# One change to a transformer layer on one core: later groups' normed x transposed by blocks, TensorE at work on ones while x loads, fewer first loads, stores in the residual's order, states 256 wide

## The chip, the core and the metric

The kernel runs on one core of one Trainium2 chip. The core has five engines with a queue each: TensorE (matmuls, written PE in the profile, its weight loads PEld), VectorE (DVE), ScalarE (ACT), GpSimd (POOL) and SyncE (SP), which here only issues DMAs. TensorE writes to PSUM[...]; all other data is in SBUF or in DRAM. The metric is the device time of one launch in microseconds. Before the change the median of 3 runs is 1242.43 us (1240.35 to 1243.34).

## The reference

One layer of attention and one feed-forward block work on the same normed x, and both are added to x. B, T, D = 8, 256, 256, with H = 16 heads of 128, M = 64 states per head, and an MLP of 2048 whose weights come as 4-bit codes with scales.

```python
xn = layernorm(x)                                   # 8 x 256 x 256
# attention
q, k = rope(xn @ Wq.T), rope(xn @ Wk.T);  v = xn @ Wv.T
s = clip(xn @ Ws1.T @ Ws2.T + bs2, -32, 32)         # low rank: 256 -> 16 -> 16 heads x 64 states
z = cumlogsumexp(s, over time);  es, enz = exp(s), exp(-z)
A = where(causal, q @ k.T * scale, 0)
ok = enz * (A @ es);  qv = softmax(ok, over states)
W2 = where(causal, (qv * enz) @ es.T, 0)
o = W2 @ v
o = o * rsqrt(mean(o * o) + eps) * g_norm_weight * silu(xn @ Wg.T)
attn = o @ Wo.T
# feed-forward
gate, up = xn @ dequant(gate_W).T, xn @ dequant(up_W).T
ffn = (gelu_tanh(gate) * up) @ dequant(down_W).T
return x + attn + ffn
```

All arithmetic is in float32.

## The kernel before

The 2048 tokens are cut into four groups of 512 (two sequences each, `g`). A step `n` is one group and one pair of heads, so there are 32 steps, run in order; a step takes about 36 us. While step n's scores, values, gates and logits are made, step n - 1 is finished (its cross terms, weights, outputs) and step n + 1 is prepared (rope and states). The feed-forward block is spread over all steps: `ffn` (L430) is a generator that gives, for each quarter of the MLP and each group, four pairs of gate and up blocks (L370, L376 and L398) and then two down products (L423).

The order on each engine is written out by a planner inside the kernel. For each step the functions are put on a list with a place in the step (`POS`, `START` for the first steps), and called in that order; a call issues its TensorE instructions at once, and hands the work of the other engines to a chain. A small clock model (`advance`, L114) with estimated durations decides in which order the chains' pieces are issued on VectorE, ScalarE, GpSimd and SyncE. `DUE` says how many pieces of the MLP's weights are unpacked by which step, `FIRST` and `LAST` how much feed-forward work the first and last steps get. None of this waits at run time: what runs is five fixed queues, each in order, tied by semaphores.

Names and lines that matter here:

- `norm` (L244): mean and variance on VectorE (L254, L255, L256), the power -1/2 on GpSimd (L258), z = normed x (L261). It is done in two halves per group, of 256 tokens each.
- `norm_turn` (L272): four transposes of a half on TensorE against the identity (L279), copied by ScalarE into xT (L289). xT is what all projections read. `NORMS` says in which step a later group is normed: group 1 in step 0, group 2 in step 2, group 3 in step 5. Group 2 and 3's x is loaded by `load_x` at the start of their step.
- `low_rank` (L481, matmuls L487) and `states` (L499, matmuls L515). rT holds four copies of the 16 low-rank rows and a row of ones in the four quarters of the partitions, and w_s2 four copies of the weights with the bias row, so four matmuls with 17 rows each can run beside each other. Each of four PSUM banks gets two matmuls of 128 columns. VectorE clips them into esT and es (L526).
- `rope` (L548, matmuls L556), `value` and `gate` (`vg`, L605, matmuls L613), `scores` (L632, L635), `logits` (L652), `softmax` (L672).
- `turned` (L450): a transpose of blocks. VectorE transposes 32x32 blocks (L453), four DMAs write the blocks to their places in DRAM (L457, `by_way`), and one DMA reads them back (L462). It is used for ok, its softmax and the outputs.
- `cross` (L723, copied by L732), `weights` (L748, masked into wt by L758), `apply` (L775, reads what L732 copied), `outputs` (L791), `close` (L841). `weights` and `apply` are two entries of the list, at 0.182 and 0.257 of a step.
- `add_to` (L345): adds a product to the residual `res` (L349). After the last addition to two tiles of 128 tokens it stores them, by eight DMAs of 32 KB (L356), since x was loaded with its rows in another order than the output's.
- The first loads, on two queues: x in two parts, the first projection weights, ws1, one_at, cos, sin and four copies of w_s2, of 17 rows each (L224 to L232); the packed weights of the MLP follow (L303, L304).

## Time and profile before

| what | value |
|---|---|
| median of 3 runs | 1242.43 us |
| the profiled execution | 1241.07 us |
| its span, first to last instruction | 1239.3 us |
| mean granted TensorE clock | 0.988 |
| first TensorE instruction | 7.10 us |
| end of the last addition to the residual | 1233.26 us |
| L556, L613, L376, L398, L423, L841 (128 x 128 weights) | 248.7, 237.0, 121.2, 123.1, 122.0, 115.7 us busy |
| DMA | 115.15 MB, mean 93 GB/s |

The profile is of one execution. Busy times of matmuls overlap a little, since they are pipelined; from one start to the next a pass of 512 columns takes 0.43 us in the middle of the run and one of 128 columns 0.107. Each float32 matmul shows as two passes (the count behind x), a transpose as one. A line such as `PE ps L279 <- DVE z L261: 16.8, 3, 7.1` says that TensorE sat idle before its instructions of line 279 for 16.8 us in all, 3 times, 7.1 us at most, until an instruction of VectorE at line 261 that writes z was done.

### The profile page before, as it was taken

To read this page: it belongs to the slowest core of one execution; us is meant where nothing else is said; L and a number is where in the kernel's file an instruction comes from. 1 tells how busy PE (TensorE), PEld (TensorE's weight loads), DVE (VectorE), ACT (ScalarE), POOL (GpSimd) and SP (SyncE) were. 2 spreads that over 40 slices of the span, in tenths; PEclk is the share of its full clock that TensorE was granted. 3 is DMA by queue.
4 is the path that set the end of the run, shared out by engine and by line. 5 is a ranking of instruction groups with operands and counts; after the bars stand their busy time and mean duration, and the time that the engine had idled before them with its cause. 6 is when DMAs were issued, how large, how long until landed. Compare 5 with 4: busy or idle time off the path is not lost.

```text
span 1239.3 us, 18558 instructions
## 1 busy us (share of the span) xinstructions
PE 1202.6 (97%) x6192; PEld 838.2 (68%) x6192; DVE 891.9 (72%) x1720; ACT 516.0 (42%) x1653; POOL 484.7 (39%) x440
## 2 busy tenths in 40 slices
PE   6899899999999999999999999899999999999996
PEld 3466586766767667767776676676766767667774
DVE  4988668868686887767777777777677586776643
ACT  3335335444354443543444443345434354442430
POOL 3525444424244433434443343444244344433310
PEclk9989999999999999999999999899999999999998
DMA  5234332324343233333332334322233333333322
GB/s 157 86 103 120 95 110 75 107 58 119 96 118 94 62 85 93 103 101 96 108 85 80 94 86 119 85 77 83 63 103 102 86 102 85 90 83 102 86 69 51
DMA packets 111495, 115.15 MB, mean 93 GB/s; under 512 B 13156, under 2 KB 83172, under 8 KB 111400
## 3 DMA queue, kind: packets, MB, share of 16 engines
q1 hardware_dynamic: 110968, 113.71, 34.2%
q8 instruction: 49, 0.80, 0.3%
q14 instruction: 46, 0.38, 0.1%
q10 hardware_dynamic: 432, 0.26, 0.1%
HBM read 78.27 MB, written 35.65 MB: 92 GB/s over the span
## 4 chain that ended last, share of the span: by engine, by line
PE 86%; DVE 9%; DMA 2%; issue 1%; POOL 1%; ACT 0%; POOLq 0%; DVEq 0%; SPq 0%; ACTq 0%
PE ps L556 16%; PE ps L613 15%; PE ps L423 9%; PE ps L841 9%; PE ps L376 8%; PE ps L398 7%; PE ps L632 4%; PE ps L791 4%; PE ps L652 4%; PE ps L748 3%; PE ps L635 2%; PE ps L515 2%; PE ps L775 1%; DVE enz L543 1%; DMA pk<-in_codes_dram 1%
## 5 line engine op out<-in xcount | busy, mean ns | idle before, releaser
L571 POOL TENSOR_TENSOR z<-z,sin 128x512 f32<-128x512 f32 x128 | 165.6, 1294 | 370.8 <-ACT z L567 369.5
L556 PE MATMUL ps<-xT,wts 128*128 128x512 f32 x512 | 248.7, 609 | 0.5 <-ACT xT L289 0.5
L613 PEld LDWEIGHTS ps<-wts,xT 128*128 128x128 f32 x1024 | 194.3, 190 | 64.1 <-issue 37.6
L613 PE MATMUL ps<-wts,xT 128*128 128x256 f32 x1024 | 237.0, 379 | 0.2
L556 PEld LDWEIGHTS ps<-xT,wts 128*128 128x128 f32 x512 | 92.1, 192 | 79.6 <-issue 69.8
L423 PE MATMUL ps<-w_down,inter 128*128 128x256 f32 x512 | 122.0, 392 | 9.4 <-DVE inter L407 7.4
L695 ACT ACTIVATE ok<-okT,mx 128x64 f32<-128x64 f32 x256 | 85.6, 337 | 91.2 <-DVE mx L689 86.6
L398 PE MATMUL ps<-xT,w_up 128*128 128x512 f32 x256 | 123.1, 604 | 0.0
L376 PE MATMUL ps<-xT,w_gate 128*128 128x512 f32 x256 | 121.2, 596 | 0.0
L572 POOL TENSOR_TENSOR q<-q,z 128x512 f32<-128x512 f32 x64 | 81.5, 1273 | 94.8 <-DVE q L569 69.7
L423 PEld LDWEIGHTS ps<-w_down,inter 128*128 128x128 f32 x512 | 98.9, 196 | 26.4 <-DVE inter L407 9.7
L841 PE MATMUL ps<-w_o,ogT 128*128 128x256 f32 x512 | 115.7, 379 | 0.0
L349 DVE TENSOR_TENSOR res<-ps,res 128x512 f32<-128x512 f32 x64 | 44.0, 688 | 93.9 <-PE ps L423 57.7
L841 PEld LDWEIGHTS ps<-w_o,ogT 128*128 128x128 f32 x512 | 96.5, 190 | 20.5 <-issue 8.1
L543 DVE RECIPROCAL enz<-enz 128x128 f32<-128x128 f32 x128 | 108.5, 909 | 0.0
L817 DVE SCALAR_TENSOR_TENSOR og<-ps,ss,sgate 128x128 f32<-128x128 f32 x256 | 75.3, 344 | 45.9 <-POOL ss L813 45.9
L566 ACT COPY z<-ps 64x512 f32<-64x512 f32 x128 | 74.5, 582 | 73.0 <-PE ps L556 63.8
L813 POOL TENSOR_TENSOR ss<-ss,nhalf 128x4 f32<-128x4 f32 x64 | 65.0, 1017 | 91.6 <-DVE ss L809 90.5
L572 POOL TENSOR_TENSOR k<-k,z 128x512 f32<-128x512 f32 x64 | 82.6, 1290 | 20.6 <-DVE k L569 16.9
L385 POOL TENSOR_SCALAR t<-t 128x512 f32<-128x512 f32 x64 | 40.7, 637 | 119.7 <-ACT t L383 116.2
L389 ACT ACTIVATE t<-t 128x512 f32<-128x512 f32 x64 | 40.2, 629 | 108.1 <-DVE t L387 108.0
L623 DVE TENSOR_TENSOR at<-ps,mask 128x384 f32<-128x384 f32 x128 | 65.4, 552 | 26.4 <-PE ps L635 26.0
(76 smaller groups left out, 1904.7 us busy)
## 6 DMA issues: line engine op xcount, KB each, us to landing
wts<-in_wqkvg_dram SPq DMA_DIRECT2D x64, 512.0 KB, 4.1
by_way<-ok SPq DMA_DIRECT2D x256, 64.0 KB, 1.8
okT<-by_way SPq DMA_DIRECT2D x64, 256.0 KB, 2.7
by_way<-og SPq DMA_DIRECT2D x256, 64.0 KB, 2.2
ogT<-by_way SPq DMA_DIRECT2D x64, 256.0 KB, 3.7
pk<-in_codes_dram SPq DMA_DIRECT2D x12, 256.0 KB, 4.3
sc<-in_scales_dram SPq DMA_DIRECT2D x12, 256.0 KB, 4.1
w_o<-in_wo_dram SPq DMA_DIRECT2D x4, 512.0 KB, 7.4
```

Source lines behind the costliest of these rows:

```text
L376: nc.tensor.matmul(pg, lhsT=w_gate[:, c, ns], rhs=xT[:, c, gs], start=c == 0, stop=c == 1)
L398: nc.tensor.matmul(pu, lhsT=w_up[:, c, ns], rhs=xT[:, c, gs], start=c == 0, stop=c == 1)
L423: nc.tensor.matmul(ps[:, k, :], lhsT=inter[g, n][0][:, (i + k) * P : (i + k + 1) * P], rhs=w_dn[:, n, :], start=n == 2 * q, stop=n == 2 * ...
L543: nc.vector.reciprocal(r, r)
L556: nc.tensor.matmul(ps, lhsT=w[:, c, :], rhs=xT[:, c, g * G : (g + 1) * G], start=c == 0, stop=c == 1)
L566: nc.scalar.copy(z[0:64], pv[64:128])
L571: nc.gpsimd.tensor_tensor(z, z, sin_b, ALU.mult)
L572: nc.gpsimd.tensor_tensor(y, y, z, ALU.add)
L613: nc.tensor.matmul(ps[:, k, :], lhsT=xT[:, c, tt], rhs=w[:, which, c, :], start=c == 0, stop=c == 1,)
L695: nc.scalar.activation(pr[:, js, i, :], okT[:, js, i, :], AF.Exp, bias=mx[:, k : k + 1], scale=SCALE, accum_out=sm[:, k : k + 1],)
L817: nc.vector.scalar_tensor_tensor(og[:, :, k, :], po[:, k, :].rearrange("p (c k) -> p c k", c=4), ss[:, k : k + 1], sg[:, k, j * DK : (j + ...
L841: nc.tensor.matmul(ps[:, k, :], lhsT=ogT[hh][0][:, i + k], rhs=w_o[:, (hp // 2) * 4 + hh, :], start=hh == 0, stop=hh == 3,)
```

## The change

- Only group 0 is still transposed on TensorE. The norm of groups 1 to 3 writes its result in blocks (four VectorE instructions of half the width in place of two), VectorE transposes the blocks, and six DMAs take them through DRAM into xT: four into `by_way`, two out of it. `turned` is split, and its first part, `scattered`, serves both. The norm stands earlier in its step (`NORM_AT`).
- VectorE sets `ones` first, and 18 matmuls of ones by ones stand ahead of all else on TensorE. Nothing reads their result.
- The first loads: ws1, one_at and gw come as one tensor (`small`), cos and sin as one (`turns`), and w_s2 as one of 128 rows, its four copies laid out on the host. All are on SP's queue.
- A store is one DMA of 256 KB: the output keeps the order of the residual's rows, and the host puts the rows in order.
- `states` makes two matmuls of 128 columns for two of the four banks, and one of 256 columns for each of the other two.
- `apply` is called at the end of `weights`, and no longer at a place of its own.
- The planner's places, due times and shares are other ones.

In the built program TensorE has 3042 matmul instructions in place of 3112 (24 transposes and 64 matmuls of states fewer, 18 on ones more), and SP issues 8 stores in place of 64 and 36 DMAs more for the six halves of the later norms; the first use of a later group's xT is the first L376 of that group, as before.

```diff
@@ -28,32 +28,33 @@
 SCALE = DK ** -0.5
 GELU_C = 0.7978845608028654
 GELU_A = 0.044715
-
-
-POS = {'scores': (0.057, 0.067),
+WARM = 18
+
+
+POS = {'scores': (0.053, 0.063),
  'logits': (0.14,),
- 'softmax': (0.303,),
+ 'softmax': (0.301,),
  'cross': (0.15,),
- 'weights': (0.182, 0.257),
- 'low': (0.024,),
+ 'weights': (0.169,),
+ 'low': (0.046,),
  'states': (0.167,),
- 'outputs': (0.364, 0.398),
+ 'outputs': (0.364, 0.472),
  'close': (0.348, 0.396),
  'rope': (0.197, 0.336, 0.411, 0.543),
- 'vg': (0.502, 0.566, 0.766, 0.838)}
-START = {-1: {'states': (0.437,), 'rope': (0.143, 0.267, 0.533, 0.633)},
- 0: {'vg': (0.0, 0.03, 0.06, 0.076),
-     'scores': (0.115, 0.195),
-     'states': (0.403,),
-     'logits': (0.318,),
+ 'vg': (0.502, 0.663, 0.838, 0.869)}
+START = {-1: {'states': (0.437,), 'rope': (0.128, 0.358, 0.518, 0.588)},
+ 0: {'vg': (0.0, 0.03, 0.076, 0.214),
+     'scores': (0.082, 0.162),
+     'states': (0.386,),
+     'logits': (0.216,),
      'softmax': (0.433,),
-     'rope': (0.198, 0.211, 0.24, 0.458)}}
-FEED = {-1: (0.301, 1.0)}
+     'rope': (0.211, 0.24, 0.245, 0.458)}}
+FEED = {-1: (0.244, 1.0)}
 NORMS = {0: 1, 2: 2, 5: 3}
-NORM_AT = (0.366, 0.78, 0.889, 0.92)
-FIRST = [0.29, 1.41]
-LAST = [1.6, 1.98]
-DUE = [4, 6, 7, 7, 8, 9, 10, 10, 11, 12, 12, 13, 14, 15, 15, 16, 17, 17, 18, 19, 19, 22, 23, 23, 24]
+NORM_AT = (0.204, 0.465)
+FIRST = [0.29, 1.5]
+LAST = [1.49, 1.82]
+DUE = [4, 6, 7, 7, 8, 9, 10, 11, 11, 11, 12, 13, 14, 15, 15, 16, 17, 17, 18, 19, 19, 22, 23, 23, 24]
 
 
...
@@ -181,13 +182,13 @@
     mask = const.tile([P, 3 * P], F32, tag="mask", name="mask")
     tri, ones = mask[:, 0:P], mask[:, P : 2 * P]
     nhalf = const.tile([P, TC], F32, tag="nhalf", name="nhalf")
-    cos = const.tile([P, T], F32, tag="cos", name="cos")
-    sin = const.tile([P, T], F32, tag="sin", name="sin")
-
-    w_s1 = const.tile([P, 2, P], F32, tag="w_s1", name="w_s1")
+    turns = const.tile([P, 2, T], F32, tag="turns", name="turns")
+    cos, sin = turns[:, 0], turns[:, 1]
+
+    small = const.tile([P, 258], F32, tag="small", name="small")
+    w_s1 = small[:, 0:256].rearrange("p (c f) -> p c f", c=2)
+    one_at, gw = small[:, 256:257], small[:, 257:258]
     w_s2 = const.tile([P, H * M], F32, tag="w_s2", name="w_s2")
-    one_at = const.tile([P, 1], F32, tag="one_at", name="one_at")
-    gw = const.tile([P, 1], F32, tag="gw", name="gw")
     w_o = const.tile([P, H, D], F32, tag="w_o", name="w_o")
     w_gate = const.tile([P, 2, MLP], F32, tag="w_gate", name="w_gate")
     w_up = const.tile([P, 2, MLP], F32, tag="w_up", name="w_up")
@@ -221,17 +222,14 @@
             wts[n, k] = w
             loads((n, k), 512)
 
+    nc.vector.memset(ones, 1.0)
     load_x(0, 2)
     load_x(2, 2)
-    nc.scalar.dma_start(out=w_s1.rearrange("p c f -> p (c f)"), in_=a["ws1"])
     load_w(0, 0)
-    nc.scalar.dma_start(out=one_at, in_=a["one_at"])
-    nc.scalar.dma_start(out=cos, in_=a["cos"])
-    nc.sync.dma_start(out=sin, in_=a["sin"])
-    for r in range(0, P, 32):
-        nc.sync.dma_start(out=w_s2[r : r + 17, :], in_=a["ws2"])
+    nc.sync.dma_start(out=small, in_=a["small"])
+    nc.sync.dma_start(out=turns.rearrange("p k t -> p (k t)"), in_=a["turns"])
+    nc.sync.dma_start(out=w_s2, in_=a["ws2"])
     make_identity(nc, ident)
-    nc.gpsimd.memset(ones, 1.0)
     make_upper_triangular(nc, mask[:, 0:P])
     make_upper_triangular(nc, mask[:, 2 * P : 3 * P])
     nc.gpsimd.memset(nhalf, -0.5)
@@ -256,16 +254,39 @@
             nc.vector.tensor_scalar(rstd, mv[:, :, 1], EPS, None, ALU.add)
             yield "g", 1.0
             nc.gpsimd.tensor_tensor(rstd, rstd, nhalf[:, 0:2], ALU.pow)
-            yield "v", 0.9
+            if g == 0:
+                yield "v", 0.9
+                for i in range(2):
+                    nc.vector.tensor_scalar(
+                        xn[:, i, :], res[:, g * TC + h + i, :], mv[:, i, 0:1],
+                        rstd[:, i : i + 1], ALU.subtract, ALU.mult,
+                    )
+                return
+
+            bl = xn.rearrange("p i d -> p (i d)").rearrange("p (q c r k) -> p q c r k", q=4, c=2, r=2)
             for i in range(2):
-                nc.vector.tensor_scalar(
-                    xn[:, i, :], res[:, g * TC + h + i, :], mv[:, i, 0:1],
-                    rstd[:, i : i + 1], ALU.subtract, ALU.mult,
-                )
-
-        xns[g, h] = xn, chain(
-            work(), st, mv, rstd, xn, rank=0, at=landed["x", g * TC + h]
-        )
+                yield "v", 0.6
+                for c in range(2):
+                    nc.vector.tensor_scalar(
+                        bl[:, :, c, i, :],
+                        res[:, g * TC + h + i, c::2].rearrange("p (q k) -> p q k", q=4),
+                        mv[:, i, 0:1], rstd[:, i : i + 1], ALU.subtract, ALU.mult,
+                    )
+            by_way = yield from scattered(bl.rearrange("p q c r k -> p q (c r) k"))
+            yield "d", 0.8, 4.2
+            for c in range(2):
+                nc.sync.dma_start(
+                    out=xT[:, c, g * G : (g + 1) * G].rearrange("p (i x) -> p i x", i=4)[
+                        :, :, 32 * h : 32 * h + 64
+                    ],
+                    in_=by_way[:, :, 64 * c : 64 * (c + 1)],
+                )
+
+        c = chain(work(), st, mv, rstd, xn, rank=0, at=landed["x", g * TC + h])
+        if g == 0:
+            xns[g, h] = xn, c
+        else:
+            normed.setdefault(g, []).append(c)
 
     xns = {}
 
@@ -349,13 +370,11 @@
         nc.vector.tensor_tensor(r, ps, r, ALU.add)
         done[t] = done.get(t, 0) + 1
         if done[t] == left:
-            yield "d", 0.9
-            for k in (t, t + 1):
-                rows = out[k // TC * G : (k // TC + 1) * G].rearrange("(i r k) d -> r i k d", i=4, r=4)
-                for i in range(4):
-                    nc.sync.dma_start(
-                        out=rows[k % TC, i], in_=res[32 * i : 32 * (i + 1), k, :]
-                    )
+            yield "d", 0.4
+            nc.sync.dma_start(
+                out=out[t * P : (t + 2) * P, :].rearrange("(i p) d -> p i d", p=P),
+                in_=res[:, t : t + 2, :],
+            )
 
     def decoded(k):
 
@@ -447,8 +466,8 @@
 
 
 
-    def turned(to, t):
-        yield "v", 0.8
+    def scattered(t):
+        yield "v", 0.7
         flat = t.rearrange("p c i k -> p (c i k)")
         nc.vector.transpose(flat, flat)
         yield "d", 1.75, 2.6
@@ -458,17 +477,16 @@
                 out=by_way.rearrange("(c k) r x -> r k c x", c=4)[r],
                 in_=t[32 * r : 32 * (r + 1)].rearrange("p c i k -> p c (i k)"),
             )
+        return by_way
+
+    def turned(to, t):
+        by_way = yield from scattered(t)
         yield "d", 0.4, 4.2
         nc.sync.dma_start(
             out=to.rearrange("p r i k -> p (r i k)"), in_=by_way.rearrange("p r x -> p (r x)")
         )
 
-    def blocks_of(t):
-
-        return t.rearrange("p (i c k) -> p c i k", i=TC, c=4)
-
     def load_wo():
-        nc.sync.dma_start(out=gw, in_=a["gw"])
         for h in range(0, H, 4):
             nc.sync.dma_start(out=w_o[:, h : h + 4, :], in_=a["wo"][:, h : h + 4, :])
 
@@ -506,15 +524,20 @@
         esT = to["esT"] = new(p2, [P, G], "esT", 2)
 
         pss = [bank() for _ in range(4)]
+        toks, sts = [rT[32 * r : 32 * r + 17] for r in range(4)], [w_s2[32 * r : 32 * r + 17, ms] for r in range(4)]
         for i in range(2):
             for r, ps in enumerate(pss):
-                rows = slice(32 * r, 32 * r + 17)
-                k = 2 * (r % 2) + i
-                tok, st = rT[rows, k * P : (k + 1) * P], w_s2[rows, ms]
-                lhsT, rhs = (tok, st) if r < 2 else (st, tok)
-                nc.tensor.matmul(
-                    ps[:, i * P : (i + 1) * P], lhsT=lhsT, rhs=rhs, start=True, stop=True
-                )
+                if r < 2:
+                    k = 2 * r + i
+                    nc.tensor.matmul(
+                        ps[:, i * P : (i + 1) * P], lhsT=toks[r][:, k * P : (k + 1) * P],
+                        rhs=sts[r], start=True, stop=True,
+                    )
+                elif i == 0:
+                    nc.tensor.matmul(
+                        ps[:, 0:T], lhsT=sts[r], rhs=toks[r][:, (r - 2) * T : (r - 1) * T],
+                        start=True, stop=True,
+                    )
 
         enz = to["enz"] = new(p2, [P, G], "enz", 2)
 
@@ -760,6 +783,7 @@
                 )
 
             to["wt", j] = wt, chain(work(), wt, pss[j], rank=0)
+        apply(n)
 
     def apply(n):
 
@@ -849,6 +873,10 @@
     banks = NG * (MLP // P * 2 + 8)
     weight = FIRST + [1.0] * (N + 2 - len(FIRST) - len(LAST)) + LAST
     feeding = ffn()
+
+    ps = bank()
+    for _ in range(WARM):
+        nc.tensor.matmul(ps[:, 0:P], lhsT=ones, rhs=ones, start=True, stop=True)
     for m in range(2):
         load_packed(m)
     load_w(0, 2)
@@ -869,10 +897,11 @@
         def put_norm(g, places):
             for k, h in enumerate((0, 2)):
                 put_at(places[k], norm, g, h)
-                put_at(places[2 + k], norm_turn, g, h)
 
         if n == -1:
-            put_norm(0, (0.0, 0.0, 0.1, 0.1))
+            put_norm(0, (0.0, 0.0))
+            for h in (0, 2):
+                put_at(0.1, norm_turn, 0, h)
             put_at(0.2, low_rank, 0)
         if n + 1 < N:
             if n >= 0 and steps[n][1] == 7:
@@ -902,7 +931,6 @@
         if n > 0:
             put("cross", 0, cross, n - 1)
             put("weights", 0, weights, n - 1)
-            put("weights", 1, apply, n - 1)
             for k in range(2):
                 put("outputs", k, outputs, n - 1, k)
             if n % 2 == 1 and n > 1:
@@ -961,18 +989,20 @@
     cos, sin = _tables()
     n = {k: np.asarray(v) for k, v in x.items()}
     at, ff = "L0_attn_", "L0_ffn_"
+    ws1 = n[at + "Ws1"].T.reshape(P, 2, 1, 16)
+    ws1 = np.pad(ws1, [(0, 0)] * 3 + [(0, 16)]).repeat(4, 2).reshape(P, 256)
+    bias = (np.arange(P) % 32 == 16).astype(np.float32).reshape(P, 1)
+    ws2 = np.concatenate([n[at + "Ws2"].T, n[at + "bs2"].reshape(1, H * M)])
+    ws2 = np.pad(ws2, [(0, 15), (0, 0)])
     return {
         "x": c(n[at + "hidden_states"].reshape(NG, 4, 4, 32, D).swapaxes(1, 2).reshape(NTOK, D)),
         "wqkvg": pairs([n[at + w] for w in ("Wq", "Wk", "Wv", "Wg")]),
         "wo": c(n[at + "Wo"].T.reshape(H, DK, D).transpose(1, 0, 2)),
-        "ws1": c(np.pad(n[at + "Ws1"].T.reshape(P, 2, 1, 16), [(0, 0)] * 3 + [(0, 16)]).repeat(4, 2).reshape(P, 256)),
-        "one_at": (np.arange(P) % 32 == 16).astype(np.float32).reshape(P, 1),
-        "ws2": c(np.concatenate([n[at + "Ws2"].T, n[at + "bs2"].reshape(1, H * M)])),
-        "gw": c(n[at + "g_norm_weight"].reshape(DK, 1)),
+        "small": c(np.concatenate([ws1, bias, n[at + "g_norm_weight"].reshape(DK, 1)], 1)),
+        "ws2": c(np.concatenate([ws2] * 4)),
         "codes": quarters(lambda w: w, "_W_packed"),
         "scales": quarters(lambda w: w.repeat(16, 0), "_scales"),
-        "cos": c(cos),
-        "sin": c(sin),
+        "turns": c(np.concatenate([cos, sin], 1)),
     }
 
 
@@ -990,4 +1020,5 @@
     with tile.TileContext(nc) as tc:
         layer_kernel(tc, aps, out)
     r = run_bass_kernel_spmd(nc, [arrays], core_ids=[0])
-    return r.results[0]["out_0_dram"].reshape(B, T, D)
+    o = r.results[0]["out_0_dram"].reshape(NG, 4, 4, 32, D).swapaxes(1, 2)
+    return np.ascontiguousarray(o).reshape(B, T, D)
```

## The prediction

> **What bounds the kernel now.** I read the page's busy times first, then the waits of TensorE, then the timeline of TensorE at each wait, and last the end of the run. The page gives the bound and the share of it:
>
> ```profile
> PE 1202.6 (97%) x6192; PEld 838.2 (68%) x6192; DVE 891.9 (72%) x1720; ACT 516.0 (42%) x1653; POOL 484.7 (39%) x440
> ```
>
> From about 80 us to 1212 us TensorE has almost no gap: there only fewer or cheaper TensorE instructions pay. What is lost beside that is in a few places, and the waits of TensorE name them (us in total, times, longest):
>
> ```profile
> PE ps L279 <- DVE z L261: 16.8, 3, 7.1
> PE ps L423 <- DVE inter L407: 7.4, 5, 2.6
> PE ps L515 <- DMA w_s<-in_ws_dram: 2.2, 1, 2.2
> ```
>
> The timeline of TensorE shows where (start, length, line; behind it the idle time before):
>
> ```profile
> 7.10 2.25 PE L279 MATMUL ps<-ident,z 128*128 128x128 f32 x8 [7.10 <-DVE z L261]
> 9.81 3.78 PE L556 MATMUL ps<-xT,wts 128*128 128x512 f32 x4 [0.46 <-ACT xT L289]
> ...
> 63.58 1.23 PE L279 MATMUL ps<-ident,z 128*128 128x128 f32 x4 [5.15 <-DVE z L261]
> ...
> 139.58 1.09 PE L279 MATMUL ps<-ident,z 128*128 128x128 f32 x4 [4.58 <-DVE z L261]
> ```
>
> TensorE stands in order, so a transpose whose z is late holds all behind it. Each long wait also slows the clock afterwards: four passes over 512 columns take 1.72 us from start to start in the middle of the run, but 3.58 us at 9.81 and 3.41 us at 64.61; the windows give a granted clock of 0.78 between 57.80 and 73.55 us and 0.84 between 134 and 145 us.
>
> **Part by part.**
>
> *Start.* Before, TensorE is first busy at 7.10 us. 18 matmuls on ones (36 passes of 128 columns) now run from about 1 us, after one memset on VectorE. What does the clock make of them? The row: first work at 7.10, half speed in every pass until about 13.9 us, so some 6.8 us of work with gaps. [...] A slow pass is 0.214 us and a fast one 0.107 (half and full rate of the 0.43 us per 512 columns). [...] by the row near 1.0 + 6.8 + 4 x 0.107 = 8.2 us, which makes the first transposes 1 us late. The second half's z ends at 8.38 either way, so both lead to a first L556 at about 9.4 (0.4 earlier) and fast from there. I take the row's side for the finish and full speed after it: 0.4 + 3.58 - 1.72 = 2.3 us, and some 0.4 of L487.
>
> The w_s2 load is now one of 128 rows and not four of 17. Those four hold SP's queue: its rows show it waiting 2.9, 2.6, 2.6 and 2.5 us for them, one after the other, and the packed weights issued behind them at 5.24 us reach VectorE only at 20.36. The new loads ahead of L515 are 1.9 MB; at the 221 to 267 GB/s of the first 10 us, an estimate of 9 us for w_s2 and 11 us for the first packed weights (2.2 MB and its scales). So the 2.2 us wait at 19.87 goes, with the slow clock behind it. By TensorE's own work the states then end at 9.4 + 4 passes + 4 passes (L487) + 4 passes + 0.65 = 15.2 us and not 20.48.
>
> What is late next is VectorE. From 20.36 to 73.5 us it is busy almost throughout (15.43 of 15.57 us, then 21.51 of 21.75, then 15.48 of 15.75), and 73.5 is when the fourth inter lets the first L423 run. Its order in the changed program has the same work before that point, plus two stream transposes (0.70 each) and smaller norm pieces (about 0.6): 2 us more. It comes to the clip of esT (before: 22.57) at 15.3, 7.2 us earlier. So the first L423 moves by 7.2 - 2.0 = 5.2 us. The 5.15 us wait at 63.58 goes as a wait on L279 but comes back as waits on VectorE inside this stage. If VectorE were no bound, TensorE's sum would allow about 15. **I take 5**, bounds 2 and 15.
>
> *Group 2's transpose.* At 139.58 the wait (4.58) and the slow clock (L632 1.06 against 0.60, and a clock of 0.84 over 11 us: 1.8) go: 6.4 at most. xT comes by VectorE, SP and DRAM; its readers are gate blocks of a later step, and the program's only waits on these DMAs stand at the first L376 of each group. VectorE has 47 of 60 us busy before it, so 1.4 + 0.6 us more can hide, but not all of the time won: **5.5**, bounds 3 and 6.4. The transposes themselves: group 3 shows 254.32 to 255.27, 0.95 us without a wait, so **1.9** for groups 2 and 3.
>
> [...] xT is now written in runs of 256 B. The near rows: okT<-by_way, 256 KB in 2 KB runs, lands in 2.7 us, by_way<-ok, 64 KB in 512 B runs, in 1.8. By the row 128 KB costs about 2 us[...]; the first reader of group 1 is at 96.04 before, and z of its second half is there at 63.8. [...] It costs elsewhere: in SP's queue the four z and two xT issues stand ahead of okT (0.44 each), so the first softmax comes some 3 us later. prT of step 0 was done at 75.5 and wanted at 78.45; I count 0, bound 3 lost.
>
> *apply joined to weights.* Not in the change's name, but in its diff, and it meets every step. Before, another matmul group stands between L748 and L775, except once at the end:
>
> ```profile
> 1164.14 1.16 PE L748 MATMUL ps<-prT,esT 64*128 64x128 f32 x16
> 1165.24 1.98 PE L398 MATMUL ps<-xT,w_up 128*128 128x512 f32 x4
> 1167.15 0.71 PE L775 MATMUL ps<-cross,prT 64*128 64x128 f32 x8
> 1167.80 3.72 PE L841 MATMUL ps<-w_o,ogT 128*128 128x256 f32 x16
> ...
> 1199.87 1.16 PE L748 MATMUL ps<-prT,esT 64*128 64x128 f32 x16
> 1200.86 0.61 PE L775 MATMUL ps<-cross,prT 64*128 64x128 f32 x8
> 1201.41 1.98 PE L398 MATMUL ps<-xT,w_up 128*128 128x512 f32 x4
> ```
>
> Apart, from start to start: 1.10 + (1.91 - 1.72) + 0.65, and 0.1 in the group behind: 2.05. Together: 0.99 + 0.55 + 0.1 = 1.64. So 0.41 us a step, 31 times: 12.7. But the order makes a new wait. The L556 behind the joined pair takes a PSUM bank that the first esT clip frees, and this clip waits for the last L748, because esT is overwritten:
>
> ```profile
> 1133.36 1.16 PE L748 MATMUL ps<-prT,esT 64*128 64x128 f32 x16
> ...
> 1134.60 0.76 DVE L526 TENSOR_SCALAR esT<-ps 128x256 f32<-128x256 f32 x2 [0.77 <-PE ps L748]
> ```
>
> The clip starts 1.24 after L748 and takes 0.42: free at 1.66, seen by TensorE at about 1.73, where the joined pair is through at 1.53. So 0.2 us of wait in 30 steps, with all of TensorE queued behind: 12.7 - 6.1 = **6.6**. Bounds: 12.7 if the wait is absorbed, 0 if VectorE comes 0.4 later. ACT's copy of cross ends 0.17 us before L748 starts, so L775 itself waits for nothing.
>
> *States 256 wide.* Two of four row groups take one matmul of 256 columns for two of 128; the groups run beside each other[...]. Columns per group stay: 0, bounds -3 and +3 over 32 steps.
>
> *Positions and due times.* At 792 us TensorE waits 1.93 and 1.95 us for VectorE before L423, and runs slow after (L423 x10 takes 4.49 instead of about 2.2). Before, this down stood 2.56 us of TensorE work behind its last up block; in the changed order it stands 5.1. A later one falls from 11.1 to 2.56. I take **3**, bounds 0 and 5. The last down still follows its up block at once, so the 3.7 us of waits at 1213 to 1217 stay.
>
> *Stores.* The end:
>
> ```profile
> 1229.83 7.31 SPq L356 DMA_DIRECT2D out_dram<-res  x16
> 1232.57 0.69 DVE L349 TENSOR_TENSOR res<-ps,res 128x512 f32<-128x512 f32 x1 [2.76 <-PE ps L841]
> ```
>
> The last sum ends at 1233.26, eight issues of 0.45 follow, and the last lands 1.6 us after its issue: 6.0 us to the end. One store of 256 KB takes one issue and lands in 2.7 to 4 us (okT, ogT, x of that size): 3.1 to 4.5. **2.3 gained**, bounds 1.5 and 2.9. Earlier stores end beside TensorE work.
>
> *Sum:* 5 + 5.5 + 1.9 + 6.6 + 0 + 3 + 2.3 = 24.3 us. The profiled execution took 1241.07 us (span 1239.3), which gives 1216.8; the runs' median is 1242.43, 1.4 above. I predict **1217**.
>
> **Rivals.**
> 1. *VectorE is no bound in the first 70 us.* Then the start gives some 13 and not 5, and the rest stays: 1209. For it: part of VectorE's busy time there is stretched (L328 x4 in 3.72 us, 0.25 each at best), which may not recur. Against it: three windows at 98 to 99%. Chance 0.22.
> 2. *The joined pair pays nothing,* since the clip's wait eats the 0.41: 1224. For it: VectorE often has another 0.68 us operation between the transpose of ok and this clip. Against it: VectorE idled 0.3 to 0.77 us before the clip. Chance 0.17.
> 3. *The new wait decides and the kernel is slower.* It becomes so when each L556 starts more than 0.7 us beyond the split form's cost, 17.7 + 3.7 us over 30 steps, that is 2.65 us after L748. The wt pair (1.28 us) ahead of the clip would do it: 30 x 1.28 = 38 us more, 1255. The order shows the clip ahead of wt in all steps that I read. Chance 0.04.
> 4. *The matmuls on ones don't open the clock:* 2 us, and VectorE's bound hides part: 1218, inside the forecast.
>
> **How the numbers follow.** Forecast 0.57, own range 1209 to 1225. With the rivals, and the bounds of the start and of the joined pair, 1204 to 1229 holds 8 in 10. A measurement of this kernel tells 0.3% (3.7 us) from no change. Faster 0.94, same 0.02, slower 0.04.
>
> **What would show it.** Right: no line waits on the transposes but once; the first L423 near 68 us; L775 directly behind L748 and about 0.2 us idle before the next L556, put down to esT; the last landing 3 to 4.5 us after the last sum; no PE wait at 140. Wrong: first L423 at 73 or at 60; waits of PE on esT of 0.6 us or more; new waits on xT or prT DMAs; long waits before L423 elsewhere.

## The result, and the profile after

The changed kernel takes 1224.72 us (median of 4 runs, 1222.62 to 1225.44) against 1242.58 (1240.35 to 1243.34) for the kernel before, whose three runs above are among its four here: ratio 0.9856, 95% interval 0.9839 to 0.9874. That is faster by 17.9 us. The profiled execution took 1225.03 us with a span of 1223.3, so between the two profiled executions the gain is 16.0 us, in the time and in the span alike. The forecast was 1217, its sum 24.3 us.

The page's line of busy times, after:

```profile
PE 1191.8 (97%) x6076; PEld 841.9 (69%) x6076; DVE 905.0 (74%) x1739; ACT 511.4 (42%) x1641; POOL 483.2 (40%) x439
```

TensorE is busy 10.8 us less, the 7.0 us of passes on ones included, and for the same 97% of the span. Its waits after (us in total, times, longest):

```profile
PE ps L655 <- POOL k L595: 8.7, 3, 5.3
PE ps L442 <- DVE inter L426: 4.2, 2, 2.5
PE ps L442 <- DVE w_down L355: 4.1, 1, 4.1
PE ps L799 <- DVE esT L549: 1.7, 5, 0.3
```

The 16.8 us of waits for z before the transposes are gone (7.1 of them were at the start, where TensorE now works on ones). In their place stand waits of the scores (L655) for the k that rope gives (L595), 8.7 us, and of the first down (L442) for decoded weights. TensorE's timeline shows the start, and the place where group 2's transposes waited before:

```profile
1.03 7.04 PE L879 MATMUL ps<-mask 128*128 128x128 f32 x36 [1.03 <-DVE mask L225]
7.92 1.11 PE L300 MATMUL ps<-ident,z 128*128 128x128 f32 x8
9.56 1.98 PE L579 MATMUL ps<-xT,wts 128*128 128x512 f32 x4 [0.53 <-ACT xT L310]
...
138.47 1.22 PE L655 MATMUL ps<-q,k 128*128 128x256 f32 x2 [5.26 <-POOL k L595]
```

The passes after the ones run fast from 9.56 us on (1.98 us for four, where it was 3.78). At 138.47 there is still a wait of 5.3 us, of another function on another engine, and the granted clock is half from 136.56 to 143.39 us. In the profiles before and after, the eight stretches of half clock that end before the run does last 3.41 us (three of them) or 6.83 (five); I call 3.41 us a window. A window of half clock in which TensorE is busy throughout costs some 1.7 us, an estimate: half of 3.41.

To see where the 16 us came from, I compared the start of the `cross` passes of each step, corrected for the feed-forward passes that one kernel had already done more than the other (0.43 us for 512 columns, 0.216 for 256). It compares one profiled execution of each:

| stretch (us, before) | gained | forecast for it |
|---|---|---|
| to 77 (start, group 1) | 3.8 | 5 |
| 77 to 148 (group 2) | -1.2 | 5.5, half of the 1.9, 0.4 of the 6.6 |
| 148 to 766 (group 3 among it) | 2.7 | 3.6 of the 6.6, the other half of the 1.9 |
| 766 to 804 (a down) | 7.0 | 3 with the next row, 0.2 of the 6.6 |
| 804 to 949 (a down) | -2.4 | 0.8 of the 6.6 |
| 949 to TensorE's end | 3.2 | 1.5 of the 6.6 |
| the stores behind it | 3.0 | 2.3 |

The end of the run, after:

```profile
1216.83 3.84 SPq L374 DMA_DIRECT2D out_dram<-res  x2
1219.56 0.69 DVE L370 TENSOR_TENSOR res<-ps,res 128x512 f32<-128x512 f32 x1 [2.76 <-PE ps L865]
```

The last sum ends at 1220.25 us and the span at 1223.3: 3.05 us, where it was 6.03.

### The profile page after: what moved, and what is told of

Read it like the earlier page. It is cut to its first block, busy times and chain, and to the rows that moved or that the text cites. A ratio compares the mean times of both kernels' runs of the same rounds, so it can differ in the third digit from the quotient of the medians.

```text
span 1223.3 us, 18297 instructions
## 1 busy us (share of the span) xinstructions
PE 1191.8 (97%) x6076; PEld 841.9 (69%) x6076; DVE 905.0 (74%) x1739; ACT 511.4 (42%) x1641; POOL 483.2 (40%) x439
## 4 chain that ended last, share of the span: by engine, by line
PE 85%; DVE 10%; POOL 2%; ACT 1%; issue 1%; DMA 1%; SPq 0%; DVEq 0%; POOLq 0%
PE ps L579 16%; PE ps L636 16%; PE ps L442 9%; PE ps L865 9%; PE ps L395 8%; PE ps L417 8%; PE ps L815 4%; PE ps L655 4%; PE ps L675 3%; PE ps L771 2%; PE ps L658 2%; DVE enz L566 1%; DVE esT L549 1%; PE ps L746 1%; PE ps L532 1%
## 5 line engine op out<-in xcount | busy, mean ns | idle before, releaser
L594 POOL TENSOR_TENSOR z<-z,turns 128x512 f32<-128x512 f32 x128 | 164.4, 1284 | 242.3 <-ACT z L590 235.6
L579 PE MATMUL ps<-xT,wts 128*128 128x512 f32 x512 | 241.8, 599 | 5.7 <-DVE t L410 1.6
L579 PEld LDWEIGHTS ps<-xT,wts 128*128 128x128 f32 x512 | 93.6, 190 | 91.5 <-issue 77.2
L442 PE MATMUL ps<-w_down,inter 128*128 128x256 f32 x512 | 121.0, 390 | 8.8 <-DVE inter L426 4.2
L442 PEld LDWEIGHTS ps<-w_down,inter 128*128 128x128 f32 x512 | 98.9, 196 | 28.9 <-DVE inter L426 5.6
L595 POOL TENSOR_TENSOR q<-q,z 128x512 f32<-128x512 f32 x64 | 81.8, 1278 | 82.8 <-DVE q L592 59.8
L566 DVE RECIPROCAL enz<-enz 128x128 f32<-128x128 f32 x128 | 108.1, 905 | 0.0
L595 POOL TENSOR_TENSOR k<-k,z 128x512 f32<-128x512 f32 x64 | 82.9, 1295 | 20.9 <-DVE k L592 15.7
```

What stands on the lines that cost most here:

```text
L442: nc.tensor.matmul(ps[:, k, :], lhsT=inter[g, n][0][:, (i + k) * P : (i + k + 1) * P], rhs=w_dn[:, n, :], start=n == 2 * q, stop=n == 2 * ...
L566: nc.vector.reciprocal(r, r)
L579: nc.tensor.matmul(ps, lhsT=w[:, c, :], rhs=xT[:, c, g * G : (g + 1) * G], start=c == 0, stop=c == 1)
L594: nc.gpsimd.tensor_tensor(z, z, sin_b, ALU.mult)
L595: nc.gpsimd.tensor_tensor(y, y, z, ALU.add)
```

## Experiments

All start from the changed kernel (1224.7). The places and weights of the plan stay as they were set for it, unless an edit names them; what that costs is seen below. The ratio is to the kernel before.

| run | us | ratio, 95% interval |
|---|---|---|
| xn in its own buffers | 1231.55 | 0.9916 (0.9901 to 0.9931) |
| apply apart | 1240.55 | 0.9990 (0.9981 to 0.9999) |
| three esT buffers | 1216.22 | 0.9793 (0.9778 to 0.9807) |
| no passes on ones | 1225.60 | 0.9864 (0.9849 to 0.9879) |
| group 2's norm a step earlier | 1226.72 | 0.9884 (0.9868 to 0.9901) |
| later groups turned on TensorE | 1224.42 | 0.9861 (0.9846 to 0.9876) |
| before's feed weights | 1231.06 | 0.9914 (0.9899 to 0.9929) |
| downs a block later | 1246.09 | 1.0032 (1.0022 to 1.0041) |
| three esT, norms over two steps | 1225.78 | 0.9869 (0.9854 to 0.9883) |
| the same, and w_o scaled later | 1221.33 | 0.9831 (0.9816 to 0.9845) |
| before's first loads | 1230.45 | 0.9908 (0.9891 to 0.9924) |
| three esT, w_o scaled later | 1216.40 | 0.9800 (0.9787 to 0.9813) |

### The joined pair: apart again, and with a third esT buffer

```diff
-'weights': (0.169,)
+'weights': (0.169, 0.257)
...
-        apply(n)
...
+            put("weights", 1, apply, n - 1)
```

> The changed kernel with the apply passes at a place of their own again (0.257), as before. The prediction's step says that joining them gained 0.21 us a step (6.6 us in all): then this is 1231. The count in the two traces says otherwise: before, the two groups and the extra 0.1 us of the wide pass behind each came to 1.96 us a step; joined they take 1.90 and 0.11, since the wide pass behind them waits for the states' clip: then it is within 1.5 us of 1224.7.

```diff
-        esT = to["esT"] = new(p2, [P, G], "esT", 2)
+        esT = to["esT"] = new(p2, [P, G], "esT", 3)
...
-        it = new(ff, [P, G], "inter", 5)
+        it = new(ff, [P, G], "inter", 4)
```

> The changed kernel with three esT buffers in place of two (inter has four in place of five, to make room). Theory C: the clip of esT for the next step writes the buffer that the weights passes of this step still read, so VectorE begins it only when they end, and the pass behind the joined pair waits for it: 0.17 us in most steps, 0.43 to 0.81 in ten. With a third buffer the pair takes 1.54 us in nearly every step (1.88 on the mean now): 6 to 10 us faster than the changed kernel, near 1216. Rival D: the clip is late because VectorE is busy, not for the buffer: pair as now, time within 2 us of 1224.7; a four-buffer inter could cost up to 2 us.

Apart, the kernel loses 15.8 us, but not through the pair. 8.1 us come in step 5, where TensorE now waits 5.8 us once for the xT DMA of group 3, 3.1 in step 2; the rest is a drift of 0.17 us a step. I count the pair in each trace from its first pass to the next group, with the 0.10 us by which a wide pass behind it is longer than usual: over 32 steps 62.7 us before, 62.5 in the changed kernel, 63.8 apart again. So joining gained 0.2 us against before and 1.3 against its own split; much of the drift is in other groups. Between step 6 and step 30, L442 grows by 2.1 us, for one.

Why next to nothing is gained shows in a step of the changed kernel, in the timeline of TensorE and VectorE:

```profile
691.44 1.16 PE L771 MATMUL ps<-prT,esT 64*128 64x128 f32 x16
...
692.43 0.38 PE L799 MATMUL ps<-cross,prT 64*128 64x128 f32 x2
692.67 0.75 DVE L549 TENSOR_SCALAR esT<-ps 128x256 f32<-128x256 f32 x2 [0.29 <-PE ps L771]
...
693.15 0.71 PE L799 MATMUL ps<-cross,prT 64*128 64x128 f32 x6 [0.34 <-DVE esT L549]
...
693.79 1.55 PE L579 MATMUL ps<-xT,wts 128*128 128x512 f32 x3
```

The clip of esT (L549) begins when the last L771 has read the old esT, and now the apply passes (L799) stand waiting in the middle for its bank. In 20 of 32 steps the pair takes 1.71 to 1.73 us, in ten 1.97 to 2.35, and only in the last two, which have no states, 1.54. With a third buffer:

```profile
506.32 1.16 PE L771 MATMUL ps<-prT,esT 64*128 64x128 f32 x16
...
507.19 0.72 DVE L549 TENSOR_SCALAR esT<-ps 128x256 f32<-128x256 f32 x2
...
507.32 0.61 PE L799 MATMUL ps<-cross,prT 64*128 64x128 f32 x8
...
507.86 1.55 PE L579 MATMUL ps<-xT,wts 128*128 128x512 f32 x3
```

The clip no longer starts behind a wait for L771, and the next group starts 1.54 us after the pair began. 21 steps are so, the pair's sum falls to 57.0 us, and the kernel to 1216.2: 8.5 us faster than the changed kernel, 5.5 of it in the pair. About 3 more come at the down at 936 us, where a wait of 1.73 us is 0.94 and one of 0.46 is gone, and at the end, where the half clock at 1205 doesn't occur. That last part is chance, as the section on the hardware shows. The four-buffer inter was not tried alone. Theory C holds for the pair.

### Group 2: does the transposing by blocks pay?

```diff
-NORM_AT = (0.204, 0.465)
+NORM_AT = (0.204, 0.465, 0.8, 0.83)
...
-            if g == 0:
+            if True:
                 yield "v", 0.9
...
                 put_at(places[k], norm, g, h)
+                if g:
+                    put_at(places[2 + k], norm_turn, g, h)
```

> The changed kernel, but the later groups' x is turned as before: whole rows normed, eight transposes on TensorE, copied by ACT (norms at the new places 0.204 and 0.465, transposes at 0.80 and 0.83). It prices the first part of the change. The prediction's steps give that part 5.5 + 1.9 = 7.4 us (and what group 1 has of it): then this is 1232 or more. The count by equal work says that the stall of group 2 came back as a wait for k in step 2, so that only the transposes' own time went (about 1 us for a group): then 1226 to 1229.

1224.4: with the first part of the change undone, the time is the same, and even my lower guess was too high. On equal work the two profiles differ by 0.1 us over group 2. At group 3 the transposes on TensorE cost 0.95 us, as the prediction had it; but at the down at 936 us this run wins back 1.3, and its end happens to be without half clock. So the blocks save about 1 us at group 3, none at group 2, and it doesn't show in the time. The waits of that run and those of the changed kernel have changed places:

```profile
PE ps L300 <- DVE z L260: 11.5, 4, 6.0
PE ps L442 <- DVE inter L426: 5.1, 4, 2.5
PE ps L799 <- DVE esT L549: 1.7, 5, 0.3
```

The waits for k are gone, and TensorE waits for z again. So what holds k? In the changed kernel, in a timeline of all engines:

```profile
119.78 1.88 PE L579 MATMUL ps<-xT,wts 128*128 128x512 f32 x4
...
122.36 0.61 DVE L841 SCALAR_TENSOR_TENSOR og<-ps,ss,sgate 128x128 f32<-128x128 f32 x2 [0.46 <-POOL ss L837]
...
129.40 1.12 DVE L270 TENSOR_SCALAR z<-res,mv,rstd 128x128 f32<-128x128 f32 x4 [0.76 <-POOL rstd L256]
...
130.31 1.33 POOL L594 TENSOR_TENSOR z<-z,turns 128x512 f32<-128x512 f32 x1
...
132.38 1.27 POOL L595 TENSOR_TENSOR q<-q,z 128x512 f32<-128x512 f32 x1 [0.73 <-DVE q L592]
...
132.84 0.60 ACT L622 ACTIVATE sgate<-ps 128x512 f32<-128x512 f32 x1 [4.24 <-DVE og L841]
...
133.63 2.22 POOL L495 TENSOR_SCALAR w_o<-w_o,small 128x1024 f32<-128x1024 f32 x2
133.68 0.58 ACT L589 COPY z<-ps 64x512 f32<-64x512 f32 x1 [0.25 <-POOL q L595]
...
134.27 0.58 ACT L590 COPY z<-ps 64x512 f32<-64x512 f32 x1
...
135.80 1.27 POOL L594 TENSOR_TENSOR z<-z,turns 128x512 f32<-128x512 f32 x1
...
137.15 1.26 POOL L595 TENSOR_TENSOR k<-k,z 128x512 f32<-128x512 f32 x1
...
138.47 0.80 PE L655 MATMUL ps<-q,k 128*128 128x256 f32 x1 [5.26 <-POOL k L595]
```

TensorE had finished k's product (the first line) by 121.7; ACT copies it at 133.68. There are four suspects on these lines: the z buffer, which q's L595 reads until 133.65 because xn stands in the ring between q and k; ACT's queue, where L622 waits 4.24 us for VectorE; POOL's two scalings of w_o; and VectorE under all of them, busy 20.4 of the 22 us from 112 to 134, with no gap longer than the 0.46 and 0.76 above. The z buffer, VectorE's load and POOL's scalings were each tried; ACT's order alone was not.

```diff
-        xn = new(p2, [P, 2, D], "z", 2)
+        xn = new(p2, [P, 2, D], "z", 2) if g == 0 else new(de, [P, 2, D], "u", 2)
```

> The changed kernel, but the normed x of the later groups lies in the decoder's u buffers and not in the two z buffers that rope's copies use. Theory A: the second half's xn stands in the z ring between q and k of head 1 (q gets one buffer, xn the other, and k must wait until POOL has used q's), so k's rope product ends at 138.4 us and TensorE waits 5.3 us at 132.9 (and 3.0 us at 56). With xn elsewhere both waits fall below 1.5 us, with them the half clock at 136.6: 4 to 8 us faster than the changed kernel, near 1218. Rival B: VectorE's norm work (4.4 us in a row at 127) and POOL's scaling of w_o hold k back, whatever buffer xn has: the wait stays over 4 us and the time within 1.5 us of 1224.7.

The copy of k moves from 133.68 to 129.38 us and the wait of the scores falls to 1.2 us, but three waits of 1.1 to 1.7 us for VectorE and ACT stand before it, at values and gates between 123 and 133, and by the next step the run is 0.8 us ahead, after 0.85 behind one step before. (A wait of 1.0 us for VectorE at 124 is in the changed kernel too.) VectorE is busy 18.2 of the 21 us from 124 to 145 (14.2 in the changed kernel). So the buffer did delay the copy, but it was not what set the time. The kernel is slower by 6.8 us for another reason: group 3's xT lands later than its first reader, which waits 5.6 us.

```diff
-NORMS = {0: 1, 2: 2, 5: 3}
+NORMS = {0: 1, 1: 2, 5: 3}
```

> The changed kernel with the whole norm of group 2 (and the load of its x) one step earlier, in step 1 in place of step 2; nothing else moves. Theory G: between 112 and 134 us VectorE is full (the norm's two halves are some 9 us of it), so rope's k is 12 us behind its pass, and the scores wait 5.3 us and then run at half clock; in step 1 VectorE is busy only 26.7 us of the 33 from 73 to 106. Then the wait at 133 falls below 1.5 us and the time by 5 to 8 us, to about 1218. Rival H: the norm fills step 1 in turn, and the wait appears near 100 us: within 2 us of 1224.7.

2.0 us slower, and rival H: the wait moves with the norm, and grows to 9.9 us. On equal work step 1 loses 11.7 us, and step 2, without the norm, runs 8.7 us faster than in the changed kernel. So the stretch is late where the norm stands. On POOL, in that run:

```profile
106.60 1.26 POOL L729 TENSOR_TENSOR prT<-okT,enz 128x512 f32<-128x512 f32 x1 [6.72 <-DMA okT<-by_way]
107.82 1.26 POOL L594 TENSOR_TENSOR z<-z,turns 128x512 f32<-128x512 f32 x1
109.16 1.26 POOL L595 TENSOR_TENSOR k<-k,z 128x512 f32<-128x512 f32 x1
```

Here the rope product of k stands in POOL's order behind prT, which waits 6.7 us for okT. The prediction had a delay of okT only as a bound, "3 lost", and only for the first step.

The next two runs take the version with three esT buffers (1216.2).

```diff
-NORMS = {0: 1, 2: 2, 5: 3}
-NORM_AT = (0.204, 0.465)
+HALVES = {
+    0: ((1, 0, 0.204), (1, 2, 0.465)), 1: ((2, 0, 0.204),), 2: ((2, 2, 0.204),),
+    4: ((3, 0, 0.204),), 5: ((3, 2, 0.204),),
+}
...
-        gn = NORMS.get(n)
-        if gn:
-            if gn > 1:
+        for gn, h, place in HALVES.get(n, ()):
+            if h == 0 and gn > 1:
                 put_at(0.0, load_x, gn * TC, TC)
-            put_norm(gn, NORM_AT)
+            put_at(place, norm, gn, h)
```

> The version with three esT buffers (1216.2 us), with the norms of groups 2 and 3 spread over two steps: their first halves in steps 1 and 4, their second halves in steps 2 and 5, each at 0.204. Theory M: no single buffer or queue makes rope's k late at 133 us, but the two halves of the norm in one step, some 9 us of VectorE's work in a stretch that it fills; with one half in each of two steps the scores' wait of 5.3 us at 133 and the half clock behind it (3.4 us lost) fall below 2 us together: 4 to 8 us faster, 1208 to 1212. Rival N: the stretch is full without the norm (rope, values, gates, decode): the wait stays over 4 us or appears in step 1, 1215 to 1218.

1225.8, 9.6 us slower. Of the 9.0 us between the two profiles, 1.6 are there before the orders differ and 1.7 come at the end, with a window of half clock that the other run doesn't have; 5.7 are the edit's. The 5.3 us at 133 become 2.7, but new waits appear behind the steps that got a first half: 3.9 us before the weights passes (L771 of the changed kernel) at 108, and 3.0 before the scores at 215, with half clock after both. Theory M falls: spreading the norm over two steps only spreads the waits.

```diff
-        if n == 2:
-            for h in range(0, H, 4):
-                put_at(0.3 + 0.04 * h, scale_wo, h)
+        if 3 <= n < 3 + H // 4:
+            put_at(0.1, scale_wo, 4 * (n - 3))
```

> As the run before, and POOL's four scalings of w_o (1.1 us each) are taken out of step 2 and put one into each of the steps 3 to 6, ahead of the close that needs them. If POOL's order is part of k's lateness (two of them, 2.2 us, stand right before k's rope product at 133.6 in the changed kernel), 1 to 2 us faster than the run before; if VectorE alone is the cause, within 1 us of it.

4.5 us faster than the run before, more than expected; but of the 2.7 us between the two profiles 1.9 are there at the end of step 0 already, up to which the two do not differ, and only 0.8 come behind it. The same edit on the version with three esT buffers alone is the cleaner test:

> The version with three esT buffers (1216.2 us) and, as its only other edit, POOL's scalings of w_o one each in steps 3 to 6 and none in step 2; the order of every other engine is unchanged. In step 2 two of them (2.2 us) stand right before the rope product of k that the scores wait 5.3 us for at 133; z for it is ready some 0.9 us after the first begins. Theory Q: POOL's order is a part of the lateness, worth those 0.9 us and a little of what k waits for earlier: the wait falls to 4 to 4.5 us, 1 us faster, 1215. If a shorter wait also spares one window of half clock, up to 3 us faster, 1213. Rival: VectorE's order alone sets it: within 0.5 us of 1216.2.

The wait falls from 5.3 to 4.5 us, as theory Q said, and the time stays at 1216.4: the half clock still runs for two windows, 6.83 us. On equal work 0.5 us is gained at the place and 0.8 lost again by step 5. I read from the five runs that not one queue sets this stretch: taking away the buffer, moving the norm, spreading it and clearing POOL each changed the waiter or its place and left most of the time. That the norm's work has no room where it stands is shown by the run with group 2's norm a step earlier. Which chain would have to be shortened stays open.

### The start

```diff
-    ps = bank()
-    for _ in range(WARM):
-        nc.tensor.matmul(ps[:, 0:P], lhsT=ones, rhs=ones, start=True, stop=True)
```

> The changed kernel without the 36 passes on ones. Theory E: the first 60 us are set by VectorE's and ACT's work for the rope products, not by TensorE's clock, so the first passes run at half clock (until about 14 us) but the logits of step 1 (72.1 us) come less than 1.5 us later, and the time is within 1.5 us of 1224.7. Rival F: each microsecond of slow passes moves the whole start: about 3 us of slow work for the six to eight wide passes before 15 us, so 2.5 to 3.5 us slower, near 1228.

The logits of step 0 come 2.7 us later and those of step 1 1.9, more than theory E allows; by the end 0.4 us are left in the profiles, and the time differs by 0.9, which is within the spread of the runs. Chance is in the 1.9 too: seven other runs have the changed kernel's orders up to there, and their logits of step 1 begin at 70.6 to 72.8 us, against 72.1 in the changed kernel and 74.0 without the ones. So the passes on ones shorten the start, by some 1 to 3 us, and little of it arrives at the end.

```diff
+    nc.scalar.dma_start(out=w_s1.rearrange("p c f -> p (c f)"), in_=a["ws1"])
     load_w(0, 0)
-    nc.sync.dma_start(out=small, in_=a["small"])
-    nc.sync.dma_start(out=turns.rearrange("p k t -> p (k t)"), in_=a["turns"])
-    nc.sync.dma_start(out=w_s2, in_=a["ws2"])
+    nc.scalar.dma_start(out=one_at, in_=a["one_at"])
+    nc.scalar.dma_start(out=cos, in_=a["cos"])
+    nc.sync.dma_start(out=sin, in_=a["sin"])
+    for r in range(0, P, 32):
+        nc.sync.dma_start(out=w_s2[r : r + 17, :], in_=a["ws2"])
...
```

> The changed kernel with the first loads as before: w_s2 in four loads of 17 rows, cos and sin apart, the three small ones on their own, ACT's queue among them; the passes on ones stay. Theory O: the first loads set the clip of the states, which moved from 22.6 to 15.7 us and is the first of VectorE's unbroken work until 66 us: back to 20 us or later, and the logits of step 1 come 2 to 4 us later than 72.1: 1227 to 1229. Rival P: VectorE's work to 66 us does not begin with the states: within 1 us of 1224.7.

1230.45: 5.7 us slower, near theory O and beyond it; the logits of step 1 come 7.2 us later, at 79.3. That is 3.4 later than before the change (75.9): without the new loads the rest of the change makes the start longer. Which part of it does was not tried, and its places were set for the new loads. The timeline of the states in that run (L541 is their second half, L352 the decode, L553 the clip):

```profile
17.35 0.67 PE L541 MATMUL ps<-rT,w_s 17*128 17x256 f32 x2 [1.77 <-DMA w_s<-in_ws_dram]
...
20.40 0.76 PE L541 MATMUL ps<-rT,w_s 17*128 17x256 f32 x1 [2.39 <-DMA w_s<-in_ws_dram]
...
20.96 0.50 DVE L352 TENSOR_SCALAR u<-pk 128x256 int32<-128x256 int32 x2 [12.36 <-DMA pk<-in_codes_dram]
...
23.16 0.75 DVE L553 TENSOR_SCALAR esT<-ps 128x256 f32<-128x256 f32 x2
```

The four loads of 17 rows hold the packed weights back to 20.96 us (11.14 in the changed kernel), and VectorE stands idle for 12.4 us; the clip of the states stands behind the decode in its order.

### The downs

```diff
-FEED = {-1: (0.244, 1.0)}
+FEED = {-1: (0.301, 1.0)}
...
-FIRST = [0.29, 1.5]
-LAST = [1.49, 1.82]
+FIRST = [0.29, 1.41]
+LAST = [1.6, 1.98]
```

> The changed kernel with before's weights of the first and last steps (FIRST 0.29, 1.41; LAST 1.6, 1.98; FEED 0.301), which set how many blocks of the MLP fall on each step. Theory I: these alone set where a down stands behind its last up block: the two waits at 792 us and the half clock behind them (7 us in the count) come back, and the wait at 936 goes: 3 to 7 us slower, near 1230. Rival J: the waits depend on the other places as well: within 2 us of 1224.7.

6.3 us slower. The down of the same place (its `w_down` passes), first in the kernel before, then in that run, then in the changed kernel:

```profile
794.42 1.83 PE L423 MATMUL ps<-w_down,inter 128*128 128x256 f32 x6 [1.93 <-DVE at L623]
798.20 4.49 PE L423 MATMUL ps<-w_down,inter 128*128 128x256 f32 x10 [1.95 <-DVE inter L407]
```

```profile
787.15 1.46 PE L442 MATMUL ps<-w_down,inter 128*128 128x256 f32 x6
792.00 4.63 PE L442 MATMUL ps<-w_down,inter 128*128 128x256 f32 x10 [3.39 <-DVE inter L426]
```

```profile
790.29 3.62 PE L442 MATMUL ps<-w_down,inter 128*128 128x256 f32 x16
```

The wait and the half clock come back with the weights of the first and last steps (7.2 us on equal work), and the wait at 936 goes (2.1 won): theory I.

```diff
                 for n in blocks(q):
-                    yield from ffn_block(g, n)
+                    b = ffn_block(g, n)
+                    next(b)
                     yield
-                for i in (0, 2):
-                    ffn_down(g, q, i)
+                    for d in late:
+                        ffn_down(*d)
+                        yield
+                    late = []
+                    for _ in b:
+                        pass
                     yield
+                late = [(g, q, 0), (g, q, 2)]
...
```

> The changed kernel, but each pair of downs stands one block later, behind the first gate product of the next group, so that VectorE has 1.7 us more to finish the last up block's product. Theory K: the waits of L442 for that product (2.1 us at 936, 2.5 at 1203 less what the last down keeps, many under 1 us) and part of the 4.1 us wait for w_down at 62 go: 2 to 5 us faster than the changed kernel, 1220 to 1223. Rival L: the later downs only move the waits to the blocks behind them: within 1.5 us of 1224.7.

21 us slower, 18 of it from one place: since group 3's first gate product now stands earlier, TensorE waits for its xT, once:

```profile
254.70 3.75 PE L395 MATMUL ps<-xT,w_gate 128*128 128x512 f32 x4 [16.00 <-DMA xT<-by_way]
```

Half clock follows from 241 to 259 us. At the first downs the 4.1 us wait for w_down became 6.5 us of waiting for VectorE one block earlier. From step 6 to step 31 the loss on equal work grows by only 0.4 us: the wait at 936 goes, which gives 2.3, but other places had lost as much before. So rival L is right for the rest of the run.

## Why the prediction was right in its range and wrong in its sum

The direction and the range (1204 to 1229) held; 1224.7 is 7.7 us above the likeliest value. By its steps:

- **Start, 5: measured 3.8.** The seven other runs with these orders give 3.1 to 5.3, so 5 is not refuted. The moves were as foretold: fast passes from 9.6 us, states at 14.9, the esT clip at 15.65 (foretold 15.3), and VectorE the bound behind it (busy 49.5 of the 50.4 us from 15.65 to 66), so rival 1 does not hold. The first down came at 61.1, not 68, but waited 4.1 us for w_down at once, until 66.0. The loads make the gain (5.7 when undone), the ones little; a cost of the other parts at the start, 2 in the forecast, is seen when the loads are undone.
- **The clock.** The first pass on ones starts at 1.03 us and the granted clock opens at 6.86, 5.8 us later; in the eleven other profiles with ones it opens 3.2 to 5.7 us after the first pass. So rival 4 does not hold. I had taken 6.8 us, from before's row with its gaps, and even the longest of the twelve is below that. In the sum it matters little: the first L579 begins at 9.56 us (9.4 foretold), and at 8.8 to 9.7 in the others.
- **Group 2's transposes, 5.5, and the transposes, 1.9: measured about 0.** This step failed. I priced the removed wait and not what is late next to it; the stretch loses 1.2 us on equal work, a wait of 5.26 us for k stands at 138.47 ("no PE wait at 140" was the sign), and undoing the part leaves the time as it is. Only group 3's 0.95 us of transposes arrived. The new route itself was no cost: its reads, 128 KB in runs of 256 B, landed in 2.9 us on the median, where I took 2 from the row, and the first readers waited 0.3 us at most. I had counted VectorE's 47 busy of 60 us as room; from 112 to 134 us, around the norm, it is busy 20.4 of 22.
- **Joined pair, 6.6: measured 0.2.** This is rival 2, in its own words. The mechanism was named and the wait was mis-sized: it is 0.17 us beyond the 1.54 in most steps, but 0.43 to 0.81 in ten, 0.33 on the mean of 30 where I had 0.2; and "2.05 apart" was 1.96 in the count. The two, some 4 and 3 us, make up the loss. In six of the ten steps a part of the foretold wait stands inside L799, since its bank too comes from VectorE.
- **States, 0:** from the first states pass to the pass behind the group 0.64 us, before 0.66 (medians of 32 steps). Before, four passes start within 0.02 us in each of four rounds; one after another, its 16 passes would take 1.7 us, an estimate from 0.107 each. Right.
- **Positions, 3: the largest gain.** 7.0 less 2.4 at the downs. The last down does not keep its 3.7 us of waits: 2.5 is left of it, and one window of half clock instead of two.
- **Stores, 2.3: 3.0**, just past the bound of 2.9.

So errors of about 7 and 6 us on the high side were partly covered by some 4 us too little at the downs. That cover is luck: without it the time would be near 1229, the upper end of the range.

## What to carry to other kernels

When a wait is removed by joining groups, look for the next writer of what they read: here one more buffer for esT was worth 8.5 us, 5.5 of them in the pair, and the joining itself 0.2. Where every engine's order is planned by hand, undoing one part also upsets places that had no slack (5.6, 5.8 and 16 us at group 3's xT alone); count the steady drift per step apart from such single losses before a part is given a price.

## What the runs showed of the hardware

Two of VectorE's operations, the norm's L270 and the decode's L349, take longer beside POOL's operations over 128x512: alone 0.34 and 0.28 us on the median, with one beside them up to 1.43 and 1.40. In the changed kernel:

```profile
117.88 1.27 POOL L594 TENSOR_TENSOR z<-z,turns 128x512 f32<-128x512 f32 x1
...
118.28 2.30 DVE L270 TENSOR_SCALAR z<-res,mv,rstd 128x128 f32<-128x128 f32 x2
119.22 1.27 POOL L595 TENSOR_TENSOR q<-q,z 128x512 f32<-128x512 f32 x1
...
120.57 0.59 DVE L270 TENSOR_SCALAR z<-res,mv,rstd 128x128 f32<-128x128 f32 x2
```

The first pair takes 2.30 us, its first ending with POOL's first product and its second with POOL's second; the second pair takes 0.59. All 9 of L270's 24 instances and all 22 of L349's 48 that take over 0.45 us end 0.08 (L270) or 0.15 us (L349) after an operation of POOL over 128x512. What they take beyond 0.28 us each comes to 7.3 and 22.2 us, of which 6.3 fall before 70 us, where VectorE is the bound. VectorE's L592, L406, block transposes (L472) and reciprocals (L566) keep their length beside POOL: 0.68, 0.68, 0.71 and 0.90 us on the median, against 0.68, 0.68, 0.70 and 0.90 alone. What makes the two others longer was not shown.

While little but a load of 17 rows is moved, the DMA engines are almost idle. In the run with before's first loads, the transfers from 5 to 22 us, in 40 slices (busy share of the 16 engines in tenths, and GB/s):

```profile
DMA  9997968977998200068976108179950884000092
GB/s 468 419 376 277 205 198 308 376 198 241 304 299 308 92 29 29 19 135 279 308 270 251 48 29 89 27 248 390 378 157 22 164 313 169 24 29 24 24 96 106
```

In the slices with 0, where the engines are busy for less than a tenth, 19 to 29 GB/s flow, where the full slices have some 200 to 470; 68 KB at 27 GB/s are 2.6 us, an estimate, and SP waits 2.5 to 2.8 us for each of the four. The kernel before shows their rows, packets of 4 KB, moved one after another: 28 of them from 14.12 to 19.09 us, each starting when the one before ends, 0.16 us on the median. Why was not shown.

Whether half clock follows a short idle is in part chance. Before the last down, twelve of the fourteen profiles show a single idle of TensorE of 2.49 or 2.50 us. In the changed kernel it is this:

```profile
1205.20 7.42 PE L442 MATMUL ps<-w_down,inter 128*128 128x256 f32 x26 [2.49 <-DVE inter L426]
```

In six of the twelve a window of half clock begins within a microsecond of its end, in the other six none does. So two profiles can differ by some 1.7 us at the end alone, by the estimate for a window above.
